# Eight PSUM banks in turn for the early pieces of layer 2, in place of four

## The chip, the cores and the metric

The kernel runs on one core of a Trainium2 chip. The metric is the device time of one execution in microseconds. The median of three timed runs is given; a further execution under the hardware profiler gives the profile, and its own time stands beside its span below.

## The reference

Four layers act on x, four sequences of 256 tokens with 256 features, so 1024 tokens. A context of 1601 rows of 256 features belongs to each sequence. Each layer is a cross-attention to the context and then a feed-forward network, both with a layernorm ahead and added to x:

```
x = x + L0_xattn(ln(x), ctx, mask)   # one head of 256
x = x + L0_ffn(ln(x))                # 32 experts of width 96, the best 8 for each token
x = x + L1_xattn(ln(x), ctx)         # a decaying sum over ctx, then ln(ln(x) + summary)
x = x + L1_ffn(ln(x))                # 8 experts of width 176, the best 2, and a shared one
x = x + L2_xattn(ln(x), ctx)         # 16 heads of 128, 4 key/value heads, ctx and own tokens
x = x + L2_ffn(ln(x))                # 4 experts of width 1024, the best one
x = x + L3_xattn(ln(x), ctx)         # 32 heads of 8
x = x + L3_ffn(ln(x))                # ternary weights, rounded activations
```

What matters here is the part of layer 2's attention that does not depend on x: for each sequence and key/value head (16 units), the keys and values of the context,

```
k_ctx = rms_norm((ctx @ wk_ctx), k_norm_w)     # 1601 x 128 for each unit
v_ctx = ctx @ wv_ctx                           # 1601 x 128 for each unit
```

## The kernel before, in words

**The early pieces.** `l2_early` (line 1207 on) is a Python generator that yields the context's keys and values of layer 2 in small pieces, long before layer 2 needs them. A unit has seven product pieces and four turning pieces. A product piece takes one PSUM bank from `self.take()`, multiplies two blocks of 128 context rows by the weights of the unit (line 1241), and ScalarE copies the keys to `kr_early` (line 1248) and the values to one of seven `va_early` buffers (line 1249), from which a transfer on SP writes them to DRAM (`vd`, line 1250). After every second piece ScalarE squares the keys (line 1259, one buffer `sq_early`), and VectorE adds the squares up (line 1260). When the unit's products are done, the root and its reciprocal are taken (lines 81 and 82), and `self.scaler`, VectorE or GpSimd, multiplies the keys (line 1266). A turning piece takes a bank too, transposes four blocks of keys of the unit before (line 1275), ScalarE brings them to one of four `kT_early` buffers (line 1277), and SP writes them to DRAM (`kd`, line 1278). `kr_early` is kept twice, so a unit's products overwrite the keys of the unit before the last.

**Where they are issued.** `fill(n)` (line 110) issues the next n pieces where other work leaves TensorE idle. The numbers stand in tables at the head of the file (`F0`, `G0`, `F1`, `G1`, `LN2`, `Q2`, `C2`).

**The banks.** From the end of layer 0's attention to the start of layer 2's, PSUM is split into three pools `self.psf` with four tags of two banks each: tpf and tp in the first, gu in the second, y in the third. In layer 0's experts tpf holds `f0tph`, tp `tp_ln` and `f0tpx`, gu the products `f0gu`, y the outputs `f0y`. Layer 1's experts use tp, gu and y. The early pieces usually take tpf, two banks, in turn. In two stages `self.take` is `wide_take` (line 103), which goes between tpf and y, so four banks:

- the way back of layer 0 (`l0_add`, line 543), in which GpSimd gathers the rows of the eight experts of each token (`f0yt`, line 566, 64 gathers with 24 buffers), VectorE adds them to x (line 558) and does layer 1's attention (`l1_xattn`); `fill(G0)` stands in each of its nine steps;
- the end of layer 1's experts (line 902 on), in which GpSimd gathers the rows of two experts (`f1yt`, line 908), VectorE adds them (line 917), and `fill(G1[t])` stands in each of eleven steps.

**The order.** Every engine works through its own queue in order. The order in a queue is laid down when the kernel is built, by a planner that estimates when each instruction can start, except for instructions handed to `pin`, which keep their program order. So a change of banks can also change the order. After the second stage the three pools close, and layer 2's own pools (`a2s`, three tiles of two banks, `a2p` and `a2o`, one bank each) take over their banks. Layer 2 starts with its weights and tables (`l_qnwra` and `l_knwra`, line 1326, from transfers that ScalarE issues, line 1323), the layernorm and transpose of the first sequence (`tp_ln`, line 1345), and `prep` of the first unit: queries (`tpq`, line 1397 on), own keys and values (`tpkv`, lines 1423 to 1426), and their scaling on GpSimd (line 1442). Then the scores (`s`), exponentials (line 1487), scaling (line 1522), transposition (line 1528) and products with the values (`o`) of unit after unit follow, with `prep` of the next unit between them.

Of the kernel before, what the change touches and what calls it, by code (L numbers as in the profile page):

```python
# [11 lines left out]
F32 = mybir.dt.float32  # L12
# [11 lines left out]
P = 128  # L24
# [34 lines left out]
class Kernel:  # L59
    def __init__(self, ctx, tc, ins, out):  # L60
        self.ctx, self.tc, self.nc = ctx, tc, tc.nc
        self.i, self.out = ins, out
        self.flip = 0
        self.hold = False
        self.flip4 = False


    def evac(self, out, in_):
# [33 lines left out]

    def wide_take(self):

        self.flip4 = not self.flip4
        if self.flip4:
            return self.psf[0].tile([P, 512], F32, name="fill", tag="tpf")
        return self.psf[2].tile([P, 512], F32, name="filly", tag="y")

    def fill(self, n):  # L110

# [2115 lines left out]
```

## Time and profile before

| what | value |
|---|---|
| timed runs, median of 3 | 2524.56 us (2520.7 to 2525.68) |
| profiled execution, its own time | 2571.23 us |
| span of the profile | 2569.2 us, 47086 instructions |
| TensorE busy | 2429.6 us, 95% of the span |
| VectorE busy | 1404.4 us, 55% |
| ScalarE busy | 1310.9 us, 51% |
| GpSimd busy | 837.8 us, 33% |
| mean granted clock of TensorE | 0.973 |
| early products into `fill` (L1241) | 572 matmuls, 146.2 us |
| early products into `filly` (L1241) | 260 matmuls, 366.8 to 664.1 us |
| additions of layer 0 (L558) | 64, 413.6 to 505.4 us |
| additions of layer 1 (L917) | 16, 647.0 to 668.7 us |

In the profile PE is TensorE, PEld its weight loads, DVE VectorE, ACT ScalarE, POOL GpSimd, SP the queue from which most transfers are issued. A row of a timeline gives the start in us, the duration in us, engine, line and operation, output and inputs, the count, and in brackets how long the engine stood idle before it and which instruction released it. "remote" or "an unknown queue" stands where the release came from no instruction that the profile ties to it, "issue" where the engine waited for nothing that the profile shows. A product piece shows as eight matmul records.

### The profile page before, as it was taken

How to read it: one execution, taken by the hardware profiler on the slowest of the kernel's cores; microseconds unless marked ns; L12 is line 12 of the kernel's file. 1: busy time of each engine (PE TensorE's matmuls, PEld its weight loads, DVE VectorE, ACT ScalarE, POOL GpSimd, SP SyncE). 2: the span in 40 equal slices, each digit the busy share in tenths (PEclk: the TensorE clock that was granted, in tenths of full speed). 3: DMA queues.
4: the chain of work that ended last, by engine and by line, in shares of the span. 5: the costliest groups of instructions: out<-in, count | busy, mean ns of one | idle time of the engine just before them, and what ended most of it. 6: DMA issues, size and time to landing. Idle time of an engine off the chain costs nothing.

```text
span 2569.2 us, 47086 instructions
## 1 busy us (share of the span) xinstructions
PE 2429.6 (95%) x17607; PEld 1507.7 (59%) x17623; DVE 1404.4 (55%) x2915; ACT 1310.9 (51%) x3000; POOL 837.8 (33%) x1516
## 2 busy tenths in 40 slices
PE   8989987899989999999999999998999999999997
PEld 5777865777645555555555555565554544544553
DVE  5453534843567777777777777763324324334323
ACT  3234434533654545454545454423336766757875
POOL 1015644213345555555555555541011001011000
PEclk9999998989999999999999999998999999999998
DMA  7165574624601111111111111004310100000000
GB/s 252 49 211 163 169 151 146 216 91 138 225 18 48 48 48 48 47 47 48 47 48 48 47 48 48 9 1 176 125 56 28 35 1 28 6 1 2 6 6 5
DMA packets 96474, 188.45 MB, mean 73 GB/s; under 512 B 15401, under 2 KB 64297, under 8 KB 95050
## 3 DMA queue, kind: packets, MB, share of 16 engines
q1 hardware_dynamic: 80102, 146.50, 16.7%
q0 software_dynamic: 10416, 28.46, 4.6%
q10 hardware_dynamic: 5732, 10.49, 1.3%
q8 instruction: 143, 2.34, 0.4%
q14 instruction: 81, 0.66, 0.1%
HBM read 137.29 MB, written 48.11 MB: 72 GB/s over the span
## 4 chain that ended last, share of the span: by engine, by line
PE 84%; DVE 5%; ACT 3%; DMA 3%; issue 2%; POOL 1%; another core or an unknown queue 1%; SPq 0%; ACTq 0%; PEld 0%; POOLq 0%; DVEq 0%; PEldq 0%
PE s L77 25%; PE o L77 24%; PE fill L1241 3%; PE f2gu L77 3%; PE b L77 3%; PE f1gu L77 2%; PE acc L77 2%; PE tpq L77 2%; PE f0gu L77 2%; PE filly L1241 2%; PE tpkv L77 2%; PE av L77 2%; PE f0y L77 2%; PE f2y L77 1%; PE f1y L77 1%
## 5 line engine op out<-in xcount | busy, mean ns | idle before, releaser
L1487 ACT ACTIVATE p<-s,nmsm 128x448 f32<-128x448 f32 (+1 forms) x512 | 326.1, 643 | 381.4 <-PE s L77 247.5
L1943 ACT ACTIVATE e<-s 128x1024 f32<-128x1024 f32 (+1 forms) x448 | 404.2, 960 | 159.6 <-PE s L77 154.5
L77 PE MATMUL o<-pT,va 128*128 128x256 f32 (+2 forms) x1920 | 434.2, 379 | 9.4 <-DVE pT L1528 7.9
L77 PE MATMUL s<-kT,qT 128*32 128x448 f32 (+1 forms) x4096 | 427.3, 558 | 11.6 <-ACT kT L1459 8.2
L77 PEld LDWEIGHTS o<-pT,va 128*128 128x128 f32 (+1 forms) x1920 | 347.5, 192 | 130.4 <-issue 89.6
L1522 POOL TENSOR_SCALAR p<-p,rm 128x448 f32<-128x448 f32 (+1 forms) x512 | 323.1, 651 | 6.2
L1483 DVE TENSOR_REDUCE nmsm<-s 128x2 f32<-128x896 f32 (+1 forms) x256 | 287.5, 1123 | 7.9
L77 PE MATMUL s<-qb,kT 32*128 32x256 f32 (+1 forms) x3328 | 268.2, 405 | 13.2 <-ACT e L1943 11.0
L1528 DVE STREAM_TRANSPOSE pT<-p 128x896 f32<-128x896 f32 (+1 forms) x256 | 270.7, 1111 | 9.4 <-POOL p L1522 8.7
L77 PEld LDWEIGHTS s<-kT,qT 128*32 128x32 f32 x4096 | 120.2, 110 | 264.0 <-issue 239.0
L77 PE MATMUL o<-e,va 128*32 128x256 f32 (+1 forms) x3328 | 236.3, 392 | 1.2 <-DVE os L2040 1.2
L77 PEld LDWEIGHTS s<-qb,kT 32*128 32x128 f32 (+1 forms) x3328 | 163.4, 181 | 105.2 <-issue 75.5
L1515 POOL TENSOR_TENSOR rm<-em,tot 32x8 f32<-32x8 f32 x256 | 54.2, 212 | 400.8 <-DVE tot L1512 389.6
L1241 PE MATMUL fill<-wkc_early,ctxT 128*128 128x256 f32 (+1 forms) x572 | 146.2, 407 | 13.4 <-ACT kT_early L1277 12.6
L77 PEld LDWEIGHTS o<-e,va 128*32 128x32 f32 (+1 forms) x3328 | 90.6, 110 | 115.1 <-issue 75.0
L1970 POOL TENSOR_TENSOR x<-x,t 128x32 f32<-128x32 f32 x64 | 14.7, 251 | 439.7 <-DVE t L1965 439.7
L1480 DVE TENSOR_TENSOR s<-s,mask 128x128 f32<-128x128 f32 (+1 forms) x256 | 84.3, 330 | 104.7 <-PE s L77 92.5
L1241 PEld LDWEIGHTS fill<-wkc_early,ctxT 128*128 128x128 f32 (+1 forms) x572 | 114.4, 203 | 35.4 <-ACT kT_early L1277 14.8
L458 POOL DMA_INDIRECT f0xr<-f0xd,f0src x95 | 90.5, 953 | 70.6 <-PE f0tph L515 18.7
L1487 ACT ACTIVATION_READ_ACCUMULATOR p<-s,nmsm 128x1 f32 x512 | 101.4, 198 | 0.0
L77 PE MATMUL f2gu<-f2wgu,f2xsT 128*128 x176 | 85.5, 611 | 0.6 <-ACT f2xsT L74 0.3
L566 POOL DMA_INDIRECT f0yt<-f0yd,f0slot x64 | 62.3, 974 | 64.1 <-DVE x L558 33.4
(488 smaller groups left out, 3500.4 us busy)
## 6 DMA issues: line engine op xcount, KB each, us to landing
ctxT<-in_ctxT SPq DMA_DIRECT2D x9, 1664.0 KB
vd<-va_early SPq DMA_DIRECT2D x96, 128.0 KB
kd<-kT_early SPq DMA_DIRECT2D x48, 256.0 KB
kT<-kd SPq DMA_DIRECT2D x16, 768.0 KB
va<-vd SPq DMA_DIRECT2D x16, 768.0 KB
f0yd<-f0ys SPq DMA_DIRECT2D x95, 128.0 KB
wq<-in_l_wq SPq DMA_DIRECT2D x16, 512.0 KB
wo<-in_l_wo SPq DMA_DIRECT2D x16, 512.0 KB
```

The costliest lines, as they stand in the source:

```text
L77: self.nc.tensor.matmul(out, lhsT, rhs, start=start, stop=stop, **kw)
L458: nc.gpsimd.indirect_dma_start(out=t, out_offset=None, in_=xd[:, :], in_offset=bass.IndirectOffsetOnAxis(ap=src[:, n : n + 1], axis=0),)
L566: nc.gpsimd.indirect_dma_start(out=yt, out_offset=None, in_=yd[:, :], in_offset=bass.IndirectOffsetOnAxis(ap=slot[:, t, r : r + 1], axis=0),)
L1241: ins = nc.tensor.matmul(tp[:rows, t, :], ctxT[u // NKV2][:, k, c0 : c0 + rows], w[u % NKV2][:, k, :], start=k == 0, stop=k == 1,)
L1480: nc.vector.tensor_tensor(sv, sv, mask[:, 2 * c : 2 * c + 2, : nt - CT, :].rearrange("p n t i -> p n (t i)"), ALU.add)
L1483: nc.vector.tensor_reduce(ms[:, 0, 2 * c : 2 * c + 2], s[:, :, : nt * 32], AX.X, ALU.max, negate=True)
L1487: nc.scalar.activation(p[:, n, : nt * 32], s[:, n, : nt * 32], AF.Exp, bias=ms[:, 0, e : e + 1], accum_out=ms[:, 1, e : e + 1],)
L1515: nc.gpsimd.tensor_tensor(r[32 * a : 32 * a + 32], e[:, a], tot, ALU.mult)
L1522: nc.gpsimd.tensor_scalar(p[:, n, : nt * 32], p[:, n, : nt * 32], r[:, e : e + 1], 1.0, ALU.mult, ALU.mult)
L1528: self.pin(nc.vector.transpose(pT[:, 2 * c : 2 * c + 2, :nt, :].rearrange("p n t i -> p n (t i)"), p[:, :, : nt * 32]))
L1943: nc.scalar.activation(e[:kr, :, :n, :], s[t][:kr, :, :n, :], AF.Exp, scale=1.0 / math.sqrt(HD3))
L1970: nc.gpsimd.tensor_tensor(xt, xt, t[:, q], ALU.add)
```

## The change

`wide_take` goes round four tags in place of two: y, gu, tp, tpf. With two banks each these are all eight banks. The pieces, their number and their places in the program stay as they are. New names are `fillg` for a piece in gu and `fillt` for one in tp.

```diff
-        self.flip4 = False
+        self.flip4 = 0
...
     def wide_take(self):
 
-        self.flip4 = not self.flip4
-        if self.flip4:
-            return self.psf[0].tile([P, 512], F32, name="fill", tag="tpf")
-        return self.psf[2].tile([P, 512], F32, name="filly", tag="y")
+        self.flip4 = (self.flip4 + 1) % 4
+        n, name, tag = ((0, "fill", "tpf"), (2, "filly", "y"), (1, "fillg", "gu"), (0, "fillt", "tp"))[self.flip4]
+        return self.psf[n].tile([P, 512], F32, name=name, tag=tag)
```

## The prediction

> **What bounds the kernel now.** I read the page's forty slices first, then the list of who waited for whom inside the two stages where `wide_take` hands out banks, then the timelines of TensorE, ScalarE and VectorE there. A slice is 2569.2 / 40 = 64.2 us.
>
> ```profile
> PE   8989987899989999999999999998999999999997
> DVE  5453534843567777777777777763324324334323
> PEclk9999998989999999999999999998999999999998
> ```
>
> TensorE is nine tenths busy almost everywhere, so a microsecond in which it idles is a microsecond of the kernel unless another engine sets the end. Stage A (way back of layer 0) is 366 to 517 us, stage B (end of layer 1) 624 to 667 us, both among the thinner slices of TensorE. The waits of 355 to 517 us (engine, line, releaser: us in total, times, longest):
>
> ```profile
> POOL f0yt L566 <- DVE x L558: 33.4, 13, 14.0
> DVE ss_early L1260 <- ACT sq_early L1259: 21.0, 8, 5.0
> ACT kT_early L1277 <- remote: 18.1, 4, 7.6
> ACT kr_early L1248 <- PE fill L1241: 15.9, 14, 4.6
> PE fill L1241 <- ACT kT_early L1277: 10.8, 6, 5.4
> ```
>
> So stage A is a ring. ScalarE stands still for "remote": a transfer out of kT_early (four buffers) or va_early (seven) that has not landed. TensorE then fills its four banks and stops; afterwards ScalarE waits for TensorE, VectorE for ScalarE, and the gathers on GpSimd for VectorE. The places (timelines of stage A; ScalarE, TensorE, VectorE):
>
> ```profile
> 398.38 0.69 ACT L1277 ACTIVATE kT_early<-filly,kw_early 128x512 f32<-128x512 f32 x1 [7.60 <-remote]
> ...
> 405.45 3.78 PE L1241 MATMUL fill<-wkc_early,ctxT 128*128 128x256 f32 x8 [2.55 <-ACT kT_early L1277]
> ...
> 413.03 0.69 DVE L1260 TENSOR_REDUCE ss_early<-sq_early 128x4 f32<-128x512 f32 x1 [5.04 <-ACT sq_early L1259]
> 413.63 3.10 DVE L558 SCALAR_TENSOR_TENSOR x<-f0yt,f0gate,x 128x256 f32<-128x256 f32 x6
> ```
>
> The additions of layer 0 (L558) begin only at 413.63, behind a reduction that waits for pieces which TensorE couldn't start before 405. In stage B and at the opening of layer 2 (TensorE, then ScalarE):
>
> ```profile
> 637.71 0.63 PE L1275 MATMUL filly<-ident,kr_early 128*128 128x128 f32 x4 [2.24 <-issue]
> 639.62 3.59 PE L1241 MATMUL fill<-wkc_early,ctxT 128*128 128x256 f32 x8 [0.23 <-issue]
> 643.04 1.89 PE L1241 MATMUL filly<-wkc_early,ctxT 128*128 128x256 f32 x8
> 654.34 0.66 PE L1275 MATMUL filly<-ident,kr_early 128*128 128x128 f32 x4 [0.76 <-ACT va_early L1249]
> 711.91 6.11 PE L77 MATMUL s<-kT,qT 128*32 128x480 f32 x48 [2.99 <-ACT p L1487]
> ```
>
> ```profile
> 636.96 0.37 ACT L1248 COPY kr_early<-filly 128x256 f32<-128x256 f32 x1 [3.21 <-DVE l_qnwrb L1328]
> 708.96 0.26 ACT L1423 COPY kr<-tpkv 32x128 f32<-32x128 f32 x1 [4.58 <-PE tpkv L77]
> ```
>
> After a wait the same piece costs 3.59 us in place of 1.89: the granted clock was 0.67, 0.67 and 0.50 in the three stretches of 10 us from 380 to 410.
>
> **The change part by part.** It adds no arithmetic and removes none. Four more banks (tags gu and tp, which the experts' tiles leave idle there) let TensorE stand four more pieces ahead of ScalarE. Building both kernels moves three things besides the names of the banks: in stage B three reductions of L1260 pass ahead of the l_knwra product, which waits for a transfer until 639.78; at the opening of layer 2 the second unit's tpq and tpkv go behind score blocks; and a few transfers on SP change places.
>
> Stage A. The hold from 380 to 404.7 stays: in it ScalarE waits for transfers, not for TensorE. But TensorE can issue products 3 to 6 of the next unit inside it (four pieces, 4 x 1.73 = 6.9 us warm, at most 4 x 3.78 = 15 us at the low clock, in 14 us left after 390.6; it would be partly cold). At 405.4 ScalarE then finds them ready. Its pace with ready pieces is read at 425.92 to 429.93: five pieces and two squares in 4.0 us. Four pieces with two squares from 405.55 end near 408.9, where the second square ended at 412.99 (412.35 + 0.64): VectorE's additions start 4.1 us sooner. What follows to 517 is VectorE's own work (8.6 to 9.4 us of every 10 in most stretches from 430), so the shift carries, unless later transfer waits of VectorE eat it (2.12 + 4.06 + 3.35 + 2.25 + 1.39 = 13.2 us after 417, which may shrink or grow when writes and gathers start sooner). Bounds: 0, and 4.1 plus a third of the 13.2, some 8.5. I take 3, nearer to the shift that one row shows.
>
> Stage B. TensorE's row from 635.5 to 666.2 has 2.24 + 0.20 + 0.23 of waits, 3.59 - 1.89 = 1.70 of low clock, then 0.76 + 0.18 + 0.26: 5.4 us, all from full banks. ScalarE stays held to 636.96 behind its own issue of l_knwb; four spare pieces (three turns of 0.44, one product of 1.73: 3.1 us) cover TensorE from 635.5 to 638.5. ScalarE waited for TensorE for 0.34 + 0.43 + 1.03 + 0.61 + 0.55 + 1.08 + 1.08 = 5.1 us from 644 to 667, so it can follow; and the reductions ahead of l_knwra free the one sq_early buffer (1.35 us of ScalarE at 641.49). At the end layer 2's PSUM pools take over banks, now all eight of them used: TensorE must then wait until ScalarE has emptied the ones it takes. If ScalarE lags by three pieces, that costs 3 x 0.8 = 2.4 us. Bounds 0 and 5.4; I take 3.5.
>
> Layer 2's opening. Before, ScalarE's first exponentials stand behind copies of tpkv (4.58 us), and TensorE waits 2.99 + 0.24 for them. Afterwards score blocks come first and tpq, tpkv fill the wait. What is late next: the second unit's rows (its kr copies pass one pair of exponentials, 1.3 us), used by GpSimd's scaling at 738, behind which the second head's p (5.02 us) queues. Bounds -1.3 (a loss) and 4.6; I take 3, TensorE's own idle time.
>
> Transfers on SP: one vd passes five weight loads, one kd and one wo change places, wq, wks and the third unit's loads shift by one or two issues of 0.32 to 0.45 us. SP is idle between them and the data are used tens of us later: 0, at worst 2 x 0.45 = 0.9. At the start of layer 1 one product (1.73 us) goes ahead of tp_ln in place of one turn (0.44), inside a wait of 2.01 us for xn: 0, or 1.3 without that cover.
>
> Sum: 3 + 3.5 + 3 = 9.5 us. The profiled execution took 2571.23 us (span 2569.2), so it would give 2561.7. The timed median is 2524.56, lower by 1.8%; the stages aren't long enough for that to change the sum, so 2524.56 - 9.5 = **2515.0 us**.
>
> **Two rules against it.** The row of the clock: in the stretches from 430 to 510, with four banks taken in turn, the granted clock was 0.89 to 1.00[...]. The Trainium skill's page TensorE: Matmul & The Clock Gate, section "A second HAM failure mode: psum-queue depth-cycling", tells of a kernel that went round the banks and whose clock sank in the small gaps between groups. If it held here, each of about 20 pieces of stage B would cost 1.7 us more, +34; by the row, nothing is added, and I take the row. The same page, "HAM oscillation", says of a kernel[...] that double buffering PSUM gained next to nothing (126.6 to 125.5 us). By it stage A gives 0 and the sum is 6.5; by the row at 413.03 it gives 3. It is the ground for the first rival.
>
> **The rivals.** First, nothing to measure: the transfers set stage A whatever TensorE does, and in stage B the wait only moves to the takeover of the banks; layer 2's opening alone remains: -3, 2521.5. For it: the 18.1 us "remote", and the VectorE-bound rows after 430. Against: 15.9 us of ScalarE waiting for `fill`.
>
> Second, slower: ScalarE empties pieces in bursts, so their seven vd and four kd writes come together with the eight gathers that VectorE's earlier additions release, and land later. Its place is ScalarE's waits for "remote" in stage A, 18.1 + 5.3 = 23.4 us now (on kT_early and on kr_early); if they double, 23.4 - 9.5 = +13.9, 2538.5. It decides from 9.5 us of growth, four tenths. For it: the longest holds came while 24 gathers were out (376 to 405 us, 125 GB/s). Against: later, with eight gathers out, transfers ran at 351 GB/s (450 to 460).
>
> **How the numbers follow.** The forecast has 0.60, the first rival 0.24, the second 0.16 with whatever smaller loss in layer 2. A measurement tells about 0.2% (5 us) from no change. Faster 0.60, same 0.24, slower 0.16. The upper bounds 8.5 + 5.4 + 4.6 give 2506; upwards the range takes in the first rival and a growth of the transfer waits by some 16 us: 2531. The forecast's own range is 2506 to 2519.
>
> **What would show it.** Right: the first L558 near 409 to 410; no TensorE wait over 1 us between 625 and 655 and no 3.6 us piece there; the first exponential of layer 2 some 5 us after its first score block, with no wait for tpkv ahead of it. Wrong: "remote" waits in stage A above 30 us, L558 still near 413, or a new wait of TensorE at layer 2's first tiles.

## The result, and the profile after

The changed kernel takes **2508.9 us** (median of 8 runs, 2496.0 to 2514.2) against 2524.2 us for the kernel before (8 runs, 2520.7 to 2527.2). The ratio is 0.9943, with a 95% interval of 0.9925 to 0.996: 15.3 us, or 0.57%, faster. The forecast was 2515.0 with a range of 2506 to 2531. The profiled execution of the changed kernel took 2512.08 us, span 2510.0.

The two profiles shown first are 59 us apart, four times the timed gain. Most of that belongs to no edit: the first profiled execution of the kernel before was 47 us above its own timed median. So below, the kernel before is read from a second profile of it (span 2522.4 us), wherever it is called "before, second profile". Line numbers of the changed kernel are one less than before.

The first rows of the page after the change, in slices of 62.8 us:

```profile
PE   8989999999999999999999999989999999999997
DVE  5544638735577777777777777753334323333323
PEclk9989999899999999999999999999999999999998
```

The thin places at slices 6 to 8 and 12 of the first page are gone. The additions of layer 0 (VectorE's timeline, columns as before) now begin 18 us after the first gather (363.4 us), where the first page had 43 us:

```profile
380.43 0.69 DVE L1259 TENSOR_REDUCE ss_early<-sq_early 128x4 f32<-128x512 f32 x1 [2.73 <-ACT sq_early L1258]
381.04 3.13 DVE L557 SCALAR_TENSOR_TENSOR x<-f0yt,f0gate,x 128x256 f32<-128x256 f32 x6
```

But the second profile of the kernel before, with four banks, has the same:

```profile
381.19 0.69 DVE L1260 TENSOR_REDUCE ss_early<-sq_early 128x4 f32<-128x512 f32 x1 [2.77 <-ACT sq_early L1259]
381.79 3.09 DVE L558 SCALAR_TENSOR_TENSOR x<-f0yt,f0gate,x 128x256 f32<-128x256 f32 x6
```

In both, no wait of ScalarE for "remote" is left on the way back. The hold of 25 us on which the forecast's first term stood is a matter of where and when the program ran, not of the banks.

The end of layer 1 and its handover to layer 2, TensorE's timeline after the change:

```profile
609.23 1.89 PE L1240 MATMUL fillt<-wkc_early,ctxT 128*128 128x256 f32 x8
611.22 0.66 PE L1344 MATMUL tp_ln<-ident,xn 128*128 128x128 f32 x4
615.83 2.02 PE L1240 MATMUL fill<-wkc_early,ctxT 128*96 128x256 f32 x4 [3.95 <-ACT va_early L1248]
617.64 2.77 PE L1274 MATMUL fill<-ident,kr_early 128*128 128x128 f32 x12
620.20 2.40 PE L77 MATMUL tpq<-wq,xT 128*128 128x512 f32 x4
```

Up to 611 TensorE goes through the stage with no wait of 1 us and every full product piece at 1.89 us. Then it stands still for 3.95 us, until a copy of ScalarE (to va_early): the pieces now lie in all eight banks, and layer 2's pools can't have one until ScalarE has emptied it. What follows runs slowly: the granted clock from 616 to 620 us is 0.50. In the second profile of the kernel before, the same four steps read:

```profile
620.76 0.60 PE L1345 MATMUL tp_ln<-ident,xn 128*128 128x128 f32 x4
621.66 1.10 PE L1241 MATMUL fill<-wkc_early,ctxT 128*96 128x256 f32 x4 [0.30 <-ACT va_early L1249]
622.61 1.47 PE L1275 MATMUL fill<-ident,kr_early 128*128 128x128 f32 x12
623.92 1.88 PE L77 MATMUL tpq<-wq,xT 128*128 128x512 f32 x4
```

The opening of layer 2 after the change, TensorE, then ScalarE:

```profile
650.76 5.39 PE L77 MATMUL s<-kT,qT 128*32 128x448 f32 x48
656.09 1.98 PE L77 MATMUL tpq<-wq,xT 128*128 128x512 f32 x4
658.00 4.82 PE L77 MATMUL s<-kT,qT 128*32 128x480 f32 x48
663.05 1.82 PE L77 MATMUL s<-kT,qT 128*32 128x480 f32 x16 [0.23 <-ACT p L1486]
```

```profile
654.70 1.28 ACT L1486 ACT_TABLE_LOAD   x1 [3.04 <-DVE nmsm L1482]
655.99 0.63 ACT L1486 ACTIVATE p<-s,nmsm 128x448 f32<-128x448 f32 x1
```

The first exponential comes 5.2 us after the first score block (before: 10.4 us in the second profile, 11.1 in the first), and no copy of tpkv stands ahead of it.

**Where the time went**, from pairs of marks in the two profiles (before, second profile, 2522.4 us; after, 2510.0 us):

| stretch | before | after | difference |
|---|---|---|---|
| start to the first gather of layer 0 | 363.9 | 363.4 | -0.5 |
| way back of layer 0: first gather to first f1gu | 107.8 | 107.2 | -0.6 |
| layer 1's experts: to the last f1y | 108.3 | 107.8 | -0.5 |
| end of layer 1: to layer 2's first tp_ln | 40.8 | 32.8 | -8.0 |
| handover: to the first score block | 32.6 | 39.6 | +7.0 |
| opening: to the 32nd exponential | 60.4 | 52.1 | -8.3 |
| from there to the end | 1808.6 | 1807.1 | -1.5 |

The last row has all that follows: 954.8 us to the last exponential on both sides, then layer 2's rest and layer 3. The timed gain is 2.9 us larger than the sum of -12.4. The profiled execution of the changed kernel (2512.08 us) is the third slowest of its eight runs, 3.2 us above their median, and those runs spread over 18 us: a difference of this size is their scatter, and one profile can't place it.

### The profile page after: what moved, and what is told of

Read it like the earlier page. It is cut to its first block, busy times and chain, and to the rows that moved or that the text cites. A ratio compares the mean times of both kernels' runs of the same rounds, so it can differ in the third digit from the quotient of the medians.

```text
span 2510.0 us, 47097 instructions
## 1 busy us (share of the span) xinstructions
PE 2408.7 (96%) x17623; PEld 1499.3 (60%) x17623; DVE 1408.7 (56%) x2915; ACT 1314.2 (52%) x3000; POOL 846.2 (34%) x1516
## 4 chain that ended last, share of the span: by engine, by line
PE 82%; DVE 6%; DMA 3%; issue 3%; ACT 2%; POOL 2%; SPq 0%; ACTq 0%; DVEq 0%; POOLq 0%
PE s L77 25%; PE o L77 24%; PE f2gu L77 3%; PE b L77 3%; PE f1gu L77 2%; PE acc L77 2%; PE tpq L77 2%; PE f0gu L77 2%; PE tpkv L77 2%; PE av L77 2%; PE fill L1240 2%; DMA f0xr<-f0xd,f0src 2%; PE f2y L77 1%; PE f0y L77 1%; PE f1y L77 1%
## 5 line engine op out<-in xcount | busy, mean ns | idle before, releaser
L1240 PE MATMUL fill<-wkc_early,ctxT 128*128 128x256 f32 (+1 forms) x444 | 110.0, 399 | 6.8 <-ACT va_early L1248 4.6
L1486 ACT ACTIVATION_READ_ACCUMULATOR p<-s,nmsm 128x1 f32 x512 | 101.3, 198 | 0.0
L1240 PEld LDWEIGHTS fill<-wkc_early,ctxT 128*128 128x128 f32 (+1 forms) x444 | 86.3, 198 | 23.0 <-ACT va_early L1248 5.7
L77 PE MATMUL f0gu<-f0w,f0xsT 128*128 x380 | 78.5, 328 | 1.4 <-DMA vd<-va_early 1.1
```

The costliest lines, as they stand in the source:

```text
L77: self.nc.tensor.matmul(out, lhsT, rhs, start=start, stop=stop, **kw)
L1240: ins = nc.tensor.matmul(tp[:rows, t, :], ctxT[u // NKV2][:, k, c0 : c0 + rows], w[u % NKV2][:, k, :], start=k == 0, stop=k == 1,)
L1486: nc.scalar.activation(p[:, n, : nt * 32], s[:, n, : nt * 32], AF.Exp, bias=ms[:, 0, e : e + 1], accum_out=ms[:, 1, e : e + 1],)
```

## The experiments

**Three theories.** The first is that of the forecast: spare banks pay in both stages, and the planner's new order at layer 2's opening adds to it. The second: transfers set the way back, so banks don't matter there. The third: banks matter next to nothing, and the order at the opening is the gain. The first eight experiments ran on chips where the kernel before took 2523 to 2525 us, the last four on another one, where it took 2565 us; ratios are always to the kernel before on the same chip.

### The kernel before once more

No edit.

> The kernel before, once more, for its profile: the first one took 2571 us, 47 us above the median of its timed runs. The time: 2524, within 5 us. If the 25 us in which ScalarE stood still for 'remote' (380 to 405 us) belonged to that one execution, the way back of layer 0 (first gather to first f1gu, 146.2 us there, 107.2 us in the changed kernel) takes some 110 to 120 us here, and the first addition of layer 0 comes some 20 us after the first gather in place of 43. If such holds are usual, it takes 135 us or more again, and the timed runs are the unusual ones.

Measured: 2522.6 us, ratio 0.9994 (0.9986 to 1.0002). The way back took 107.8 us and the first addition came 17.9 us after the first gather. On these chips the hold was not there. It is not a freak either: on the chip of the last group all four kernels profiled there have it (way back 142.6 to 148.3 us). Which kind of chip the first profile of the kernel before came from is not known; its way back of 146.2 us is like those four.

### Eight banks in one stage at a time

The number of tags is set for each stage (`a_only`: 4 in the way back, 2 at the end of layer 1; `b_only`: 2, then 4). A tag has two banks.

```diff
-        self.flip4 = (self.flip4 + 1) % 4
-        n, name, tag = ((0, "fill", "tpf"), (2, "filly", "y"), (1, "fillg", "gu"), (0, "fillt", "tp"))[self.flip4]
+        tags = ((0, "fill", "tpf"), (2, "filly", "y"), (1, "fillg", "gu"), (0, "fillt", "tp"))[: self.ntags]
+        self.flip4 = (self.flip4 + 1) % self.ntags
+        n, name, tag = tags[self.flip4]
...
         take = self.take
+        self.ntags = 4
         self.take = self.wide_take
...
             self.scaler = nc.vector
+            self.ntags = 2
             self.take = self.wide_take
```

> All eight banks on the way back of layer 0, four at the end of layer 1 as before. The order at the opening of layer 2 is nearly that of before. Theory 1 (spare banks pay in both stages and the opening as well): -3 us, 2521, with the addition of layer 0 some 4 us sooner. Theory 2 (transfers set the way back, banks don't matter there): 0, 2524. If the missing 6 us of the measured -15.3 sit here: -9, 2515.

> Four banks on the way back of layer 0, all eight at the end of layer 1; the opening of layer 2 has the changed kernel's order. Theory 1: -6.5 us, 2517.5 (the changed kernel's profile puts stage B, the takeover of the banks and the opening together at 77.6 us against 86.1 us before, so -8.5 by that pair). Theory 2: all of the measured -15.3, 2509. If the missing 6 us are in the way back of layer 0: -6 to -8, 2517.

Measured: the way back alone 2513.8 us, ratio 0.996 (0.9947 to 0.9973), -11 us; the end of layer 1 alone 2505.3 us, ratio 0.9924 (0.9909 to 0.9939), -20 us. Each gives more than the first theory's share, and together they sum to twice what the change with both gave. So something else differs between these executions. The way back took 107.8 and 107.4 us: eight banks there do nothing. What differs is the stretch after it: layer 1's experts took 103.0 and 103.3 us in place of 108. The granted clock at their entry, two stretches of 10 us from the first f1gu (columns: window, length, busy TensorE and its matmuls, granted clock, DMA share, GB/s), after the change and then with eight banks in the way back alone:

```profile
470.60:480.60 10.00, 9.21 (x34) 0.52 0.90 282
480.60:490.60 10.00, 10.00 (x41) 0.79 0.26 79
```

```profile
469.90:479.90 10.00, 9.18 (x51) 0.86 0.96 324
479.90:489.90 10.00, 10.00 (x43) 0.96 0.31 90
```

### The opening of layer 2 alone

Four banks in both stages as before. The first four score blocks and the second unit's tpq keep their program order, in which the scores come first.

```diff
-                        self.mm(tqf, xb[:, k, q * P : (q + 1) * P], w["wq"][:, k, :], k == 0, k == 1)
+                        ins = nc.tensor.matmul(tqf, xb[:, k, q * P : (q + 1) * P], w["wq"][:, k, :], start=k == 0, stop=k == 1)
+                        if u == 1:
+                            self.pin(ins)
...
                             qT[:, h, q0 : q0 + 32], kT[:, :nt, 32 * a : 32 * a + 32], start=True, stop=True,
                         )
+                        if self.opening:
+                            self.pin(ins)
...
+                        self.opening = n + step < 2 and n == 0
```

> Four banks in both stages, as before, but at the opening of layer 2 the first four score blocks are held ahead of the second unit's tpq and tpkv, as in the changed kernel. Theory 1: -3 us, 2521 (first score block to first exponential 5 us in place of 11.1). Theory 3 (the banks do nothing, the order of the opening all): -15, 2509. If the opening's gain is only lent (the second unit's rows are late next): 0, 2524.

Measured: 2517.7 us, ratio 0.9973 (0.9964 to 0.9983), -7.2 us. That is more than twice the forecast's 3, without a bank more. The 32nd exponential came 55.8 us after the first score block: between the 60.4 of before and the 52.1 after the change. So the order alone gives a gain that is clear of noise. It has only part of the new order: both of the second unit's tpq go behind four score blocks here, while the changed kernel has the first one ahead of all of them.

### Eight banks with the old opening

Eight banks in both stages, but the second unit's preparation is written ahead of the first score blocks, and ScalarE's copies of tpkv and its first exponentials are kept in that order.

```diff
...
+                        self.opening = n + step == 0
+                        if self.opening:
+                            w = load(units[1][1])
+                            pieces = prep(1, w, ready)
+                            for _ in range(3):
+                                next(pieces)
                         for cc in (c, c + 1):
                             hd["p"].append(scores(kT, qT, h, cc, hd["ms"]))
...
```

> All eight banks in both stages, but the first exponentials of layer 2 are held behind the second unit's tpkv copies, as in the kernel before (the second unit's preparation is written ahead of the first score blocks, and ScalarE's copies and first exponentials keep that order). Theory 1 (the spare banks themselves are worth 6.5 us and the opening 3): some 4 to 7 us slower than the changed kernel, 2513 to 2516, with 10 to 11 us from the first score block to the first exponential. Theory 3 (the opening's order is nearly all of it): 2522 to 2524. If the opening is only lent: 2509.

Measured: 2511.6 us, ratio 0.9956 (0.9943 to 0.9968). The first exponential is late again, 11.0 us after the first score block, but the 32nd comes at 53.6 us, near the changed kernel's 52.1. Against the third theory as it was written: the first exponential's place is not what counts. The first theory's time is nearer (2513 to 2516) than the third's (2522 to 2524), but its reason isn't borne out, since the opening kept most of the new order's gain. Nor did this run bring the old order back, so it doesn't decide between the theories: in ScalarE's queue four copies of tpkv lie ahead of the first exponentials, in the kernel before it is one ahead and three behind the sixth. TensorE's granted clock was below 1.00 in two of the first six windows of 10 us (0.93 and 0.83), as after the change (0.94 and 0.83); in the second profile of the kernel before in four (0.66, 0.83, 0.92, 0.74).

Three of these windows, counted from the first score block (columns: window, length, then busy time of PE, PEld, DVE, ACT and POOL, granted clock, DMA share, GB/s), before (second profile) and after:

```profile
663.40:673.40 10.00, 8.23 (x56) 2.30 (x60) 3.22 (x6) 6.60 (x21) 0.75 (x4) 0.66 0.00 0
673.40:683.40 10.00, 8.89 (x80) 2.46 (x72) 8.10 (x14) 6.13 (x20) 5.98 (x14) 1.00 0.12 28
683.40:693.40 10.00, 8.92 (x42) 6.36 (x43) 7.93 (x18) 5.92 (x14) 2.97 (x8) 0.83 0.01 3
```

```profile
660.80:670.80 10.00, 9.77 (x88) 3.08 (x84) 8.59 (x18) 7.33 (x23) 2.61 (x8) 1.00 0.01 2
670.80:680.80 10.00, 9.36 (x62) 4.58 (x50) 9.06 (x14) 3.87 (x14) 8.30 (x17) 1.00 0.09 27
680.80:690.80 10.00, 9.01 (x69) 4.18 (x68) 5.20 (x11) 7.01 (x19) 6.76 (x13) 1.00 0.01 2
```

TensorE waits and then runs slowly. Before (second profile), then the last two of these waits after the change:

```profile
665.16 14.35 PE L77 MATMUL s<-kT,qT 128*32 128x480 f32 x112 [2.99 <-ACT p L1487]
...
684.48 5.14 PE L77 MATMUL o<-pT,va 128*128 128x256 f32 x16 [2.18 <-DVE pT L1528]
...
702.75 6.34 PE L77 MATMUL o<-pT,va 128*128 128x256 f32 x16 [3.42 <-DVE pT L1528]
```

```profile
677.44 3.46 PE L77 MATMUL o<-pT,va 128*128 128x256 f32 x16 [0.64 <-DVE pT L1527]
...
693.25 4.95 PE L77 MATMUL o<-pT,va 128*128 128x256 f32 x16 [3.44 <-DVE pT L1527]
```

After the change 48 score matmuls take 4.82 us (the row at 658.00), so 112 would take 11.2; before they took 14.35, 3.1 us more. The two o blocks took 1.7 and 1.4 us more. Over the 4 us from the start of each of these rows the granted clock was 0.50, 0.57 and 0.50 before, and 1.00 and 0.61 after.

### Two and six banks

The table of tags is cut to the first entry (`two`: tpf alone) and to the first three (`six`: tpf, y, gu), in both stages.

> Two banks only in both stages (tag tpf), with the changed kernel's order at the opening of layer 2. If the number of banks matters (theory 1), TensorE and ScalarE take turns: stage B goes from 41 us (four banks) to 46 us or more, the way back of layer 0 gets longer as well, and the time is 10 us or more above the run with only the opening changed (2517.7), 2528 or more. Theory 2 and 3 (banks are idle anyway, only the order matters): 2517, within 4 us.

> Six banks (tags tpf, y and gu) in both stages. Theory 1: two spare pieces of the four: stage B some 36 us (between 41 and 33), but the handover to layer 2's banks shorter by half of the 7 us that it grew with eight; time 2509, within 4 us, as with eight. If only the full eight cover ScalarE's stand-still at the end of layer 1: 2515. Theory 3: 2517.

Measured with two banks: 2522.0 us, ratio 0.9998 (0.999 to 1.0006). The way back took 118.7 us: eleven more than with four, six or eight, ScalarE waiting for TensorE 42 times (total, times, longest):

```profile
ACT kr_early L1250 <- PE fill L1243: 40.7, 42, 1.9
```

So the way back does need banks, but four are enough. End of layer 1 and handover together took 74.2 us, as with four (73.4). The expected 2528 was counted from the 2517.7 of the opening alone, plus the longer way back and five more for the end of layer 1. The way back came as expected. But the end of layer 1 with its handover is not longer, the opening took 51.6 us where that run has 55.8, and layer 1's experts 104.3 where it has 107.6.

Measured with six: 2505.8 us, ratio 0.9925 (0.9912 to 0.9937). End of layer 1 and handover take 34.8 + 33.9 = 68.7 us, 3.7 less than with eight. tp is left alone, and at the handover TensorE waits 0.92 us, not 3.95, and keeps its clock:

```profile
610.69 0.60 PE L1347 MATMUL tp_ln<-ident,xn 128*128 128x128 f32 x4
612.22 1.10 PE L1243 MATMUL fill<-wkc_early,ctxT 128*96 128x256 f32 x4 [0.92 <-ACT va_early L1251]
613.15 1.47 PE L1277 MATMUL fill<-ident,kr_early 128*128 128x128 f32 x12
```

### The clock at layer 1's entry

Twelve transposes that nobody reads, of the last thing that VectorE computes ahead of xn, are put in front of layer 1's first tp_ln.

```diff
+            for _ in range(12 if pool and b == 0 else 0):
+                self.nc.tensor.transpose(tp[:, 0, 0, :], self.z1[:, 1, P:], self.ident)
...
+        self.z1 = z
```

> The changed kernel with twelve transposes that nobody reads put in front of layer 1's first tp_ln, so that TensorE doesn't stand still for the 2 us until xn is there. In the profiles so far the granted clock of the 10 us after this place was 0.50 to 0.52 in three runs and 0.83 to 0.86 in the two runs whose layer 1 (first f1gu to last f1y) took 103 us in place of 108. If that stand-still costs the clock: 103 us here, and 2504 in place of 2509. If the clock falls for another reason (transfers, or the wait of 0.78 us for xnT): 108 us, and 2509 or 1 us more.

Measured: 2504.5 us, ratio 0.9924 (0.9911 to 0.9936), and 104.6 us for layer 1's experts. TensorE's wait of 2.01 us for xn is cut to 0.62 and 0.51:

```profile
467.52 1.53 PE L125 MATMUL tp_ln<-ident,z 128*128 128x128 f32 x12 [0.62 <-DVE z L1204]
469.56 1.52 PE L128 MATMUL tp_ln<-ident,xn 128*128 128x128 f32 x8 [0.51 <-DVE xn L95]
```

The time is as expected (layer 1's experts were to take 103 us), but its interval overlaps the changed kernel's, so the timed gain over it is not established.

### The new order with four banks

Only the second tag is another one: tp in place of y. No bank more, and no pin. The planner then lays down the changed kernel's order at the opening of layer 2.

```diff
-        self.flip4 = (self.flip4 + 1) % 4
-        n, name, tag = ((0, "fill", "tpf"), (2, "filly", "y"), (1, "fillg", "gu"), (0, "fillt", "tp"))[self.flip4]
+        self.flip4 = (self.flip4 + 1) % 2
+        n, name, tag = ((0, "fillt", "tp"), (0, "fill", "tpf"))[self.flip4]
```

> Four banks in turn in both stages, as in the kernel before, but the second pair is that of tag tp in place of y: no bank more. The order at the opening of layer 2 becomes that of the changed kernel (three score blocks, the second unit's tpq, four score blocks, tpkv). If that order is what the change is worth (theory 3: the 32nd exponential 52 us after the first score block in place of 60): -8 us or a little more, 2515. If the number of banks is (theory 1): -3, 2521.

The changed kernel was run again beside it, on the same chip:

> The changed kernel once more, on the same chip as the others, for its profile and its scatter. 2509, within 3 us. If the clock at layer 1's entry is a matter of the single execution: layer 1 may take 103 us here in place of 107.8; if it follows from the order of the instructions, 107 to 108 us again.

Measured on this chip: before 2565.3 us; four banks with tp 2553.7, ratio **0.995** (0.9936 to 0.9963); the changed kernel 2553.0, ratio **0.996** (0.9944 to 0.9976). Within these intervals, some 4 us each way, four banks and eight are the same. The 32nd exponential comes at 51.4 us in both. More than that: in the 50 us from the first score block, TensorE's matmuls come in one and the same order in the changed kernel and in the runs with two, four (tp) and six banks, and the stretch to the 32nd exponential takes 51.4 to 53.1 us in all of them, with or without unread transposes. It follows the order, not the number of banks. The opening with four banks:

```profile
697.98 4.82 PE L77 MATMUL s<-kT,qT 128*32 128x448 f32 x48
702.74 1.98 PE L77 MATMUL tpq<-wq,xT 128*128 128x512 f32 x4
704.65 4.82 PE L77 MATMUL s<-kT,qT 128*32 128x480 f32 x48
```

The expected times were written for a chip on which the kernel before takes 2524 us; as differences, -8 was expected and -11.5 came. The changed kernel's layer 1 took 103.4 us here, 107.8 in its first profile: the same instructions can have either outcome. The granted clock here, as the columns above:

```profile
511.30:521.30 10.00, 9.21 (x46) 0.83 0.92 298
521.30:531.30 10.00, 10.00 (x50) 1.00 0.21 65
```

Whether the chip or the single execution settles it is not shown.

### Four and six banks with the transposes

> The same four banks, with the twelve unread transposes ahead of layer 1's first tp_ln. If the two causes add up (order of the opening -8, clock at layer 1's entry -4 to -5): 2511, with layer 1 (first f1gu to last f1y) at 103 to 105 us. If the transposes only worked because eight banks had shifted the work: 2515.

> Six banks in both stages with the twelve unread transposes: the handover to layer 2's banks without the wait of 3.9 us, and the clock kept at layer 1's entry. From the stages measured one by one (way back 107.2, layer 1 103 to 104.6, stage B and handover 68.7 in place of 72.4, opening as in the changed kernel): 6 to 8 us below the changed kernel, 2501 to 2503. If the run with six banks had its gain from a lucky clock at layer 1's entry alone (103.1 us there): as with eight banks and the transposes, 2504.5.

Measured: 2552.1 us, ratio 0.9948 (0.9934 to 0.9963), and 2550.6 us, ratio 0.9943 (0.9927 to 0.9958). Layer 1's experts took 101.3 and 101.7 us, the clock at their entry 1.00 in both:

```profile
513.30:523.30 10.00, 9.67 (x58) 1.00 0.85 243
```

With four, six and eight banks, then, no profile with the transposes has the low clock of 0.50 at layer 1's entry. But five of the eleven profiles without them don't have it either, so three are not proof that the transposes do it. In the timed runs the expected steps don't show: four banks gain 1.6 us by them, and six are 2.3 us below the changed kernel where 6 to 8 were expected. On this chip the way back, 142.6 to 148.3 us, varies by more than that between single profiles. No version is shown to beat the changed kernel: six banks, the transposes, and eight banks at the end of layer 1 alone are each 3 to 4.5 us below it in their medians (2505.8, 2504.5 and 2505.3), with intervals that overlap its own.

The marks of all runs, one profile each, in us:

| run | banks: way back, end of layer 1 | way back | layer 1 | end of layer 1 | handover | to 32nd exponential | ratio |
|---|---|---|---|---|---|---|---|
| before, second profile | 4, 4 | 107.8 | 108.3 | 40.8 | 32.6 | 60.4 | 0.9994 |
| changed | 8, 8 | 107.2 | 107.8 | 32.8 | 39.6 | 52.1 | 0.9943 |
| way back alone | 8, 4 | 107.8 | 103.0 | 37.6 | 32.2 | 59.0 | 0.996 |
| end of layer 1 alone | 4, 8 | 107.4 | 103.3 | 32.6 | 39.6 | 52.1 | 0.9924 |
| opening alone | 4, 4 | 107.6 | 107.6 | 42.0 | 33.2 | 55.8 | 0.9973 |
| old opening | 8, 8 | 107.1 | 107.4 | 32.5 | 38.8 | 53.6 | 0.9956 |
| two banks | 2, 2 | 118.7 | 104.3 | 26.2 | 48.0 | 51.6 | 0.9998 |
| six banks | 6, 6 | 107.2 | 103.1 | 34.8 | 33.9 | 52.2 | 0.9925 |
| eight, transposes | 8, 8 | 107.6 | 104.6 | 32.5 | 37.8 | 51.6 | 0.9924 |
| before, first profile | 4, 4 | 146.2 | 107.5 | 41.8 | 33.2 | 58.0 | |
| changed, last group | 8, 8 | 142.6 | 103.4 | 37.3 | 37.8 | 51.4 | 0.996 |
| four with tp, last group | 4, 4 | 144.2 | 107.6 | 28.5 | 44.5 | 51.4 | 0.995 |
| four with tp, transposes | 4, 4 | 144.4 | 101.3 | 28.0 | 44.5 | 52.9 | 0.9948 |
| six, transposes | 6, 6 | 148.3 | 101.7 | 36.6 | 33.3 | 53.1 | 0.9943 |

Where tp or one tag is used alone, layer 2's first tp_ln stands earlier in TensorE's queue, so there only the sum of the end of layer 1 and the handover compares.

## Why the prediction was right in its number and mostly wrong in its steps

The forecast of -9.5 us lay near the measured -15.3, and the range held it, near its lower end. That was luck in good part: two of its three terms were too large, by 4.9 us together, and the third too small by 5.3, so the sum came out near the -9.9 of these stretches.

**Way back, -3 forecast, nothing found.** The step that failed is "The hold from 380 to 404.7 stays". On the chips of the first eight experiments there is no hold, so nothing for spare banks to shorten: TensorE's pieces keep up with four banks, and the way back took 107.8 us against 107.2. With the hold, the first addition does come earlier, 38.5 us after the first gather in place of 42.9 (4.4 us; 4.1 was forecast), and the way back took 142.6 us in place of 146.2. But four banks with tp have 37.9 and 144.2. So the banks aren't shown to do it; what does, another execution or chip or the other tag, stays open. The sign was on the page: the profiled execution was 47 us above the timed runs, and the forecast said of this that "the stages aren't long enough for that to change the sum". 38 of those 47 us lay in that one stage (146.2 against 107.8).

**End of layer 1, -3.5 forecast, -1.0 found.** The stage itself gained 8.0, more than what had been read off its waits (the parts listed there add up to 5.6, not 5.4; three of its waits show "issue", so that full banks caused them was an inference). The handover took 7.0 back. The forecast had seen it and priced it at 2.4 (three pieces of ScalarE's lag): this is the mis-sized term. Measured were a wait longer by 3.65 us (3.95 against 0.30), and the low clock after it: 2.02 - 1.10, 2.77 - 1.47 and 2.40 - 1.88, 2.7 us. Together 6.4 of the 7.0. This was listed as the sign of a wrong forecast, "a new wait of TensorE at layer 2's first tiles", and it came.

**Layer 2's opening, -3 forecast, -8.3 found.** The mechanism was right as far as it went: score blocks first, tpq and tpkv into the gaps, the first exponential 5.2 us after the first score block (5 forecast). The term that was mis-sized is "TensorE's own idle time": it counted the first wait (2.99 + 0.24) and stopped there. From the first score block to the end of the o block behind the last wait shown, 240 score matmuls, 46 of o and 16 of tpq and tpkv on both sides, TensorE took 55.7 us before and 47.4 after. Of these 8.3 us, the waits are 4.3: 2.99 + 2.18 + 3.42 = 8.6 us before, 0.23 + 0.64 + 3.44 = 4.3 after. The other 4 us are slower rows. The three rows shown above for before are 3.1, 1.7 and 1.4 us slower than after the change, at a granted clock of 0.50 to 0.57 behind the waits; some rows of the changed kernel are slower in turn. The upper bound of 4.6 us was too low for the same reason. The forecast had priced the clock in stage B (3.59 us for a piece of 1.89) and in stage A, but not here. Waits shorter than three microseconds were enough on the first page as well: from 696.1 to 700.1, behind one of 1.87 us, the granted clock was 0.67, though from 730 to 734, behind one of 2.17, it was 1.00.

**Transfers on SP and layer 1's start, 0 forecast.** Right for the changed kernel: layer 1's experts 107.8 against 108.3 us, the wait for xn 2.01 us in both.

**The two rules.** The Trainium skill's page TensorE: Matmul & The Clock Gate, section "A second HAM failure mode: psum-queue depth-cycling", puts the loss down to frequent short idle times between groups of matmuls. These did not arise here: going round eight banks at the end of layer 1, TensorE had no wait of 1 us, and every full product piece took 1.89 us. So the +34 did not come, and what the page says is not tested. The measurement in its section "HAM oscillation", no further gain from double buffering PSUM, is of a kernel already rearranged to keep TensorE busy between its transfers, so not quite this case. As a guide it was the better one: way back 0, and end of layer 1 with handover -1.0.

**The rivals.** The first one described what happens, though not its reason for the way back (no transfer holds it on the first chips): the way back doesn't care, at the end of layer 1 "the wait only moves to the takeover of the banks", and the opening alone remains. It had the same undersized 3 us for it, and so gave 2521.5. With the 8.3 that the profile shows it would have said 2516. The second rival, transfers that hold longer, is not seen: the changed kernel's way back has no "remote" wait on the chips of the first groups, and 18.0 + 5.7 = 23.7 us on the other one, as the first page had (23.4).

**What stays open.** Both profiles of the kernel before have the low clock at layer 1's entry (0.50); of the two of the changed kernel, one has it (0.52) and one doesn't (0.83). If the odds of it differ between the programs, that is part of the timed gains, and no trace shows it for the other executions. Which part of the new order at the opening counts is open as well: moving the score blocks alone gave 55.8 us, the late first exponential 53.6, the whole order 52.1. Six banks and four banks in the run with the way back alone have end of layer 1 and handover at 68.7 to 69.9 us, the other four-bank kernels at 72.5 to 75.2, and one profile each can't say which part of that is the banks. (In the run with the way back alone the two tags also come in the other order at the end of layer 1: TensorE's waits there stand before pieces in `fill`, in the kernel before in front of `filly`.) Four banks with tp and eight were compared only on the chip that has the hold.

## What to carry to other kernels

When a planner lays down the order, renaming a resource can move instructions far downstream: compare the orders, and test the order with the resource held fixed, as the four banks with tp did here. A buffer that lets TensorE run ahead of the engine that empties it pays only if the next stage doesn't need the buffer back at once; with a pair left free (six banks) that wait was 0.92 us in place of 3.95. When a profiled execution is far above the timed runs, find the stage that holds the excess before pricing anything in it.

## What the runs showed of the hardware that was not expected

**The clock at layer 1's entry came out in two ways.** Over the two stretches of 10 us from the first f1gu the granted clock was 0.50 to 0.52 and then 0.75 to 0.86, or 0.83 to 1.00 and then 0.96 to 1.00, and layer 1's experts took 107.4 to 108.3 us or, without the transposes, 103.0 to 104.3. The changed kernel had one in its first profile and the other in its second. TensorE's waits ahead of it, in the changed kernel's first profile, are 0.71, 0.18 and 2.01 us within 8 us:

```profile
461.63 0.66 PE L1274 MATMUL fill<-ident,kr_early 128*128 128x128 f32 x4 [0.71 <-ACT va_early L1248]
462.46 0.66 PE L1274 MATMUL fill<-ident,kr_early 128*128 128x128 f32 x4 [0.18 <-ACT va_early L1248]
...
468.95 1.51 PE L126 MATMUL tp_ln<-ident,xn 128*128 128x128 f32 x8 [2.01 <-DVE xn L95]
```

The Trainium skill's page TensorE: Matmul & The Clock Gate, section "What's actually happening", says that activity is counted in a window of about 3.4 us that runs freely, so the same kernel can change its clock at different points; that fits two outcomes with the same instructions, but no run here shows the window itself. With the twelve transposes the three profiles show 101.3, 101.7 and 104.6 us.

**One chip was 35 to 41 us slower in one stage.** On the chip of the last group the way back took 142.6 to 148.3 us in four profiles, on the others 107.1 to 107.8 in eight kernels out of nine (two banks: 118.7), with ScalarE waiting up to 8.2 us at a time for "remote". Whether that is the chip or the time at which it ran is not shown. The changed kernel's gain was 0.57% on the one and 0.40% on the other, which the intervals don't separate.
